# A graph-attention layer on one Trainium2 core: where the count and the report of failed rows stand, and the segment size for blocks 24 to 27

## The chip, the core and the metric

The kernel runs on one core of a Trainium2 chip. The metric is the device time of one launch in microseconds (us). Each kernel is run several times, and the median is used. One further execution is recorded by the hardware profiler. Times inside it are counted from the start of its span.

## The reference

There are 4096 nodes with 512 features. `adj` is a 4096 x 4096 matrix of f32; about one entry in 256 is not zero, and these are drawn between 0.05 and 1e9.

```python
ht = (h @ W).reshape(N, 4, 512).transpose(1, 0, 2)          # 4 heads
src = einsum('hnd,hd->hn', ht, a[:, :512, 0])
dst = einsum('hnd,hd->hn', ht, a[:, 512:, 0])
e = leaky_relu(src[:, :, None] + dst[:, None, :], 0.01) + adj[None]
h_prime = einsum('hij,hjd->hid', softmax(e, axis=-1), ht).mean(axis=0)
out = layernorm(x + h_prime)                                # over the 512 features
```

The entries of adj are added to the scores before the softmax. Where the largest entry of a row leads the second by more than the scores can make up, the softmax of that row is 1 at one column and 0 elsewhere, for all heads. The row of `h_prime` is then the row of x at that column times the mean of the four heads' W.

## The kernel before, in words

The kernel has two parts. `leading_rows` takes every row as one with such a lead, computes the output from that, and tests on the way whether the lead is large enough. `general` computes the whole attention for blocks of rows in which the test failed. A flag decides whether it is entered: `any_bad` is read by every engine at line 64, after `leading_rows`. In the profiled execution the flag is 0 and `general` does not run.

The rows are worked on in 32 blocks of 128. Row p * 32 + nb of the matrix lies in partition p of block nb. The order of the work is written out by hand: each engine executes its own instructions in the order of the source. A loop over t = 0 to 31 has a pipeline of these steps for each block:

- **Load.** SP loads the block's 128 x 4096 entries of adj (2 MB) up to five rounds ahead into one of six buffers. Blocks 28 to 30 come in two pieces and block 31 in four.
- **Segment maxima** (line 182, DVE). Each row is cut into segments of e columns, and the maximum of each segment is taken. For blocks 0 to 17 e is 16 (256 segments), for blocks 18 to 27 it is 32 (128 segments), for 28 to 31 it is 64 (64 segments).
- **Find the segment** (lines 189 and 191, DVE). MAX8 takes the eight largest segment maxima, and FIND_INDEX8 finds where they are. POOL makes a row number of it (198) and fetches that segment of adj anew from DRAM with an indirect DMA (202), into a tile named `lead`. The pool of such tiles has 8 buffers for e = 16, 8 for e = 32 and `LAST` for e = 64.
- **Find the column**, two rounds later (219 and 225, DVE). MAX8 of the fetched segment gives the second largest value inside it, and FIND_INDEX8 finds the maximum's column. For blocks 24 to 31 the MAX8 is left until after the loop. POOL adds the column up (227) and gathers the rows of x at these columns (213) into the tile y.
- **Turn and multiply**, three rounds later. PE transposes y in four pieces (240), ACT copies the result out of PSUM as yt (242), and PE multiplies it by the mean W in four steps of 128 (255). An f32 product is two passes in the profile. For blocks below 24 the block's own x is added by a product with the identity (248).
- **Layer norm and store.** ACT takes the sums for blocks 0 to 26 (277, 279), POOL makes the factor (282 to 284), ACT applies it (288). For blocks 27 to 31 DVE takes the statistics with BN_STATS (308, 312), ACT the square root (314), DVE the reciprocal (317), and DVE or ACT normalises (324, 288, 337). Blocks 24 to 27 are put by in a buffer of adj (268), and their x is added later (272).

After the loop stands the tail, a list of calls. Block 30's column (`find_column(NB - 2)`) waits for its fetched segment. Block 31's column is searched in the whole row (line 233, 4096 values). Its segment is fetched as well, but for the test alone. `test` (405 to 408) compares the lead of every row of all 32 blocks with a bound, and needs the segment of block 31. `count` (412) adds up over the partitions by a small product on PE, into a PSUM tile px. `report` is three small DVE instructions (416, 418, 419) that turn px into `n_bad` and `any_bad`. Block 31's products are made in two halves of 256 columns (297), and each half's statistics are taken as soon as it is there (331). The last store is that of block 31.

The part of the tail that the change touches reads in source order (before):

```python
    test()
    turn(NB - 2)
    ...
    products(NB - 3, KB - 1, KB)
    pg = count()
    products(NB - 2, 0, KB - 1)
    report(pg)
    moments(NB - 3)
    ...
    turn(NB - 1)
    products(NB - 2, KB - 1, KB)
```

Of the kernel before, what the change touches and what calls it, by code (L numbers as in the profile page):

```python
# [23 lines left out]
E_EARLY = 16  # L24
E_LAST = 64
EARLY = 18
LAST = 4


@with_exitstack  # L30
def gat_resnorm_kernel(
# [28 lines left out]
    any_bad = keep.tile([1, 1], I32, name="any_bad")  # L60

    leading_rows(tc, x, adj, W, a, out, ident, n_bad, any_bad)

    flag = nc.values_load(any_bad[0:1, 0:1], min_val=0, max_val=N)
# [5 lines left out]
def leading_rows(ctx, tc, x, adj, W, a, out, ident, n_bad, any_bad):  # L70
# [21 lines left out]
    lead_pool = ctx.enter_context(tc.tile_pool(name="lead_pool", bufs=1))  # L92
    LEADS = (8, 8, LAST)
    small = ctx.enter_context(tc.tile_pool(name="small", bufs=5))
# [3 lines left out]
    adj_rows = adj.rearrange("(p nb) m -> nb p m", nb=NB)  # L98
    spans = ((E_EARLY, 0, EARLY), (E, EARLY, NB - LAST), (E_LAST, NB - LAST, NB))
    adj_segs = {e: adj.rearrange("n (s e) -> (n s) e", e=e) for e, _, _ in spans}  # L100
# [135 lines left out]
    def turn(ib):  # L236
        y = y_t.pop(ib)
        tp = psum.tile([P, KB, P], F32, name="tp", bufs=2)
        for kb in range(KB):
            nc.tensor.transpose(tp[:, kb, :], y[:, ds(kb, P, KB)], ident)  # L240
        yt = yt_of[ib] = rows.tile([P, KB, P], F32, name="yt")
        nc.scalar.copy(yt, tp)  # L242
# [7 lines left out]
    def products(ib, lo=0, hi=KB):  # L250
        start = ib not in o_ps
        if start:
            o_ps[ib] = psum.tile([P, D], F32, name="o")
        for kb in range(lo, hi):
            nc.tensor.matmul(  # L255
                o_ps[ib], yt_of[ib][:, kb, :], w_sum[:, kb, :],
                start=(start and kb == 0), stop=(kb == KB - 1),
            )
# [11 lines left out]
    def add_x(engine, ib):  # L270
        o = o_ps[ib] = o_ps["by"][:, ib - BEHIND, :]
        engine.tensor_add(o, o, hold[:, ib, :])
# [13 lines left out]
    def finish(ib):  # L286
        i = slice(ib, ib + 1)
        nc.scalar.activation(hold[:, ib, :], o_ps.pop(ib), AF.Identity, bias=nm[:, i], scale=sd[:, i])  # L288
# [15 lines left out]
    def moments(ib):  # L304

        if ib < NB - 1:
            st = small.tile([P, nc.vector.BN_STATS_DIM], F32, name="st", bufs=2)
            nc.vector.bn_stats(st, o_ps[ib])
        else:
            st = halves_st  # L310
        mv = mean_var[ib] = small.tile([P, nc.vector.BN_AGGR_DIM], F32, name="mv", bufs=3)
        nc.vector.bn_aggr(mv, st)
        r = rt[ib] = sd[:, ib : ib + 1]
        nc.scalar.activation(r, mv[:, 1:2], AF.Sqrt, bias=eps)

    def factor(ib, shift=False):
        nc.vector.reciprocal(rt[ib], rt[ib])
        if shift:
            nc.vector.scalar_tensor_tensor(
                nm[:, ib : ib + 1], mean_var[ib][:, 0:1], -1.0, rt[ib], op0=OP.mult, op1=OP.mult  # L320
            )

    def normalise(ib, o, columns=slice(0, D)):
        nc.vector.tensor_scalar(
            hold[:, ib, columns], o, mean_var[ib][:, 0:1], rt[ib], op0=OP.subtract, op1=OP.mult
        )
# [3 lines left out]
    def stats_of_half(ib, k):  # L330
        nc.vector.bn_stats(halves_st[:, k, :], o_ps[ib][k])
# [78 lines left out]
    def count():  # L410
        pg = psum.tile([1, NB], F32, name="px", bufs=1)
        nc.tensor.matmul(pg, ones[:, 0:1], gap, start=True, stop=True)
        return pg

    def report(pg):
        nc.vector.tensor_scalar(n_bad, pg, -1.0, float(P), op0=OP.mult, op1=OP.add)
        total = once.tile([1, 1], F32, name="total")
        nc.vector.tensor_reduce(total, pg, axis=AX.X, op=OP.add)
        nc.vector.tensor_scalar(any_bad, total, -1.0, float(N), op0=OP.mult, op1=OP.add)
# [90 lines left out]
    stats(BEHIND + 2)  # L510
    rstd(slice(BEHIND, BEHIND + 3))
    products(NB - 3, KB - 1, KB)
    pg = count()
    products(NB - 2, 0, KB - 1)
    report(pg)
    moments(NB - 3)
    factor(NB - 3)
    normalise(NB - 3, o_ps.pop(NB - 3))
    turn(NB - 1)
    products(NB - 2, KB - 1, KB)  # L520
    add_x(nc.vector, LATE - 1)
    finish(BEHIND)
    finish(BEHIND + 1)
# [9 lines left out]
    stats_of_half(NB - 1, 0)  # L533
    factor(NB - 2)
    normalise(NB - 2, o_ps.pop(NB - 2))
    stats_of_half(NB - 1, 1)
    moments(NB - 1)
    factor(NB - 1, shift=True)
# [180 lines left out]
```

## Time and profile before

| | |
|---|---|
| median of 3 runs | 235.98 us (235.09 to 237.04) |
| the profiled execution | 235.12 us, span 233.6 us |
| PE busy | 165.8 us, 71% of the span |
| DVE busy | 199.2 us, 85% |
| ACT busy | 114.5 us, 49% |
| POOL busy | 102.0 us, 44% |
| DMA | 97.09 MB, mean 416 GB/s |
| mean granted PE clock | 0.965 of full speed |

The profiled execution took 1.5 us more than its span. A share of busy time is an average over the whole span. What holds the end is read from the chain of waits and the timelines of its last stage. In the rows, "out<-in" names what an instruction writes and reads, "x" counts instructions, and the part in brackets is the idle time of the engine before the instruction, with what ended it. PEld is PE's weight load, which runs beside the products. The ends of products are modelled, so they overlap a little; starts are the safer times.

### The profile page before, as it was taken

How to read it: one execution, taken by the hardware profiler on the slowest of the kernel's cores; microseconds unless marked ns; L12 is line 12 of the kernel's file. 1: busy time of each engine (PE TensorE's matmuls, PEld its weight loads, DVE VectorE, ACT ScalarE, POOL GpSimd, SP SyncE). 2: the span in 40 equal slices, each digit the busy share in tenths (PEclk: the TensorE clock that was granted, in tenths of full speed). 3: DMA queues.
4: the chain of work that ended last, by engine and by line, in shares of the span. 5: the costliest groups of instructions: out<-in, count | busy, mean ns of one | idle time of the engine just before them, and what ended most of it. 6: DMA issues, size and time to landing. Idle time of an engine off the chain costs nothing.

```text
span 233.6 us, 2053 instructions
## 1 busy us (share of the span) xinstructions
PE 165.8 (71%) x457; PEld 76.5 (33%) x457; DVE 199.2 (85%) x312; ACT 114.5 (49%) x284; POOL 102.0 (44%) x215
## 2 busy tenths in 40 slices
PE   0000001999978299979769689969999968999890
PEld 0000001344433244434325244324444433444360
DVE  0599999699919999999789995999999999979782
ACT  2012331055756159667547364643855644188661
POOL 2030334416424464646443552646464555457400
PEclk9999999999999679999999979988999999999997
DMA  6999999999999999999999999999999999999995
GB/s 242 434 429 428 432 408 422 435 435 420 434 422 435 419 436 422 430 422 436 426 428 431 426 428 422 425 432 426 423 436 417 425 427 424 412 423 424 422 387 219
DMA packets 11967, 97.09 MB, mean 416 GB/s; under 512 B 1960, under 2 KB 2408, under 8 KB 5936
## 3 DMA queue, kind: packets, MB, share of 16 engines
q1 hardware_dynamic: 8352, 88.08, 89.0%
q0 software_dynamic: 3584, 8.84, 9.6%
q8 instruction: 4, 0.07, 0.1%
q14 instruction: 11, 0.09, 0.1%
q10 hardware_dynamic: 16, 0.02, 0.0%
HBM read 88.54 MB, written 8.39 MB: 415 GB/s over the span
## 4 chain that ended last, share of the span: by engine, by line
POOL 34%; issue 34%; DMA 16%; DVE 9%; PE 3%; POOLq 1%; ACT 0%; SPq 0%; DVEq 0%
DMA adj_t<-in_adj_dram 11%; POOL lead L202 11%; POOL y L213 11%; DVE seg L182 6%; DMA lead<-in_adj_dram,row 5%; POOL sd L283 4%; POOL row L198 2%; POOL start L209 2%; POOL col L227 2%; PE o L255 2%; PE o L297 2%; POOL sd L282 1%; DVE col L233 1%; POOL nm L284 1%; DVE at L191 1%
## 5 line engine op out<-in xcount | busy, mean ns | idle before, releaser
L182 DVE TENSOR_REDUCE seg<-adj_t 128x128 f32<-128x2048 f32 (+3 forms) x66 | 145.4, 2207 | 21.8 <-DMA adj_t<-in_adj_dram 21.7
L255 PE MATMUL o<-w_sum,yt 128*128 128x512 f32 x248 | 118.9, 622 | 0.7 <-ACT yt L242 0.7
L255 PEld LDWEIGHTS o<-w_sum,yt 128*128 128x128 f32 x248 | 46.5, 199 | 64.6 <-issue 46.3
L240 PE MATMUL tp<-ident,y 128*128 128x128 f32 x128 | 23.1, 306 | 58.1 <-DMA y<-in_x_dram,col 57.7
L242 ACT COPY yt<-tp 128x512 f32<-128x512 f32 x32 | 18.8, 586 | 83.0 <-PE tp L240 83.0
L240 PEld LDWEIGHTS tp<-ident,y 128*128 128x128 f32 x128 | 19.1, 209 | 77.6 <-issue 75.9
L202 POOL DMA_INDIRECT lead<-in_adj_dram,row x32 | 32.7, 1022 | 15.0 <-POOL row L198 15.0
L213 POOL DMA_INDIRECT y<-in_x_dram,col x32 | 30.8, 961 | 16.9 <-POOL col L227 15.8
L248 PE MATMUL o<-hold,ident 128*128 128x512 f32 x52 | 29.4, 653 | 1.3 <-DMA hold<-in_x_dram 1.3
L198 POOL TENSOR_TENSOR row<-at,first 128x1 uint32<-128x1 uint32 x32 | 6.7, 209 | 44.7 <-DVE at L191 44.7
L227 POOL TENSOR_TENSOR col<-start,within 128x1 uint32<-128x1 uint32 x31 | 5.8, 188 | 33.5 <-DVE within L225 33.5
L262 ACT ACTIVATE sq<-hold 128x512 f32<-128x512 f32 x32 | 19.8, 619 | 0.0
L288 ACT ACTIVATE hold<-o,nm,sd 128x512 f32<-128x512 f32 x24 | 17.3, 771 | 1.2 <-POOL nm L284 1.2
L279 ACT ACTIVATE sq<-o,nm 128x512 f32<-128x512 f32 x24 | 16.5, 688 | 0.8
L277 ACT ACTIVATE sq<-o 128x512 f32<-128x512 f32 x24 | 14.4, 602 | 0.0
L347 ACT ACTIVATE w_sum<-w_sum 128x512 f32<-128x512 f32 x4 | 2.5, 629 | 20.8 <-DVE w_sum L346 20.8
L189 DVE MAX8 top<-seg 128x8 f32<-128x256 f32 (+2 forms) x32 | 11.6, 361 | 1.1
L191 DVE FIND_INDEX8 at<-top,seg 128x8 uint32<-128x256 f32 (+2 forms) x32 | 11.3, 352 | 0.0
L283 POOL TENSOR_TENSOR sd<-sd,power 128x2 f32<-128x2 f32 (+1 forms) x13 | 9.6, 735 | 1.1
L355 ACT ACTIVATE sq<-hold 128x512 f32<-128x512 f32 x16 | 9.9, 619 | 0.0
L248 PEld LDWEIGHTS o<-hold,ident 128*128 128x128 f32 x52 | 8.9, 211 | 3.0 <-DMA hold<-in_x_dram 2.5
L209 POOL TENSOR_TENSOR start<-at,width 128x1 uint32<-128x1 uint32 x31 | 6.6, 213 | 0.8
(84 smaller groups left out, 98.7 us busy)
## 6 DMA issues: line engine op xcount, KB each, us to landing
adj_t<-in_adj_dram SPq DMA_DIRECT2D x28, 2048.0 KB, 30.8
adj_t<-in_adj_dram SPq DMA_DIRECT2D x6, 1024.0 KB, 28.0
out_dram<-hold SPq DMA_DIRECT2D x6, 1024.0 KB, 17.3
hold<-in_L_gnn_W_dram SPq DMA_DIRECT2D x2, 2048.0 KB, 13.3
hold<-in_x_dram SPq DMA_DIRECT2D x2, 2048.0 KB, 37.7
hold<-in_x_dram SPq DMA_DIRECT2D x3, 1024.0 KB
adj_t<-in_adj_dram SPq DMA_DIRECT2D x4, 512.0 KB, 19.5
out_dram<-hold SPq DMA_DIRECT2D x3, 512.0 KB
```

Of the source, the lines that this page charges most:

```text
L182: nc.vector.tensor_reduce(seg_of[ib][:, ts(k, N // e // n)], adj_t[ib][:, ts(k, N // n)].rearrange("p (s e) -> p s e", e=e), axis=AX.X, op ...
L202: nc.gpsimd.indirect_dma_start(out=lead, out_offset=None, in_=adj_segs[e], in_offset=bass.IndirectOffsetOnAxis(ap=row[:, :1], axis=0),)
L213: nc.gpsimd.indirect_dma_start(out=y, out_offset=None, in_=x, in_offset=bass.IndirectOffsetOnAxis(ap=col[:, :1], axis=0),)
L240: nc.tensor.transpose(tp[:, kb, :], y[:, ds(kb, P, KB)], ident)
L242: nc.scalar.copy(yt, tp)
L248: nc.tensor.matmul(o_ps[ib], ident, hold[:, ib, :], start=start, stop=False)
L255: nc.tensor.matmul(o_ps[ib], yt_of[ib][:, kb, :], w_sum[:, kb, :], start=(start and kb == 0), stop=(kb == KB - 1),)
L262: nc.scalar.activation(sq, hold[:, ib, :], AF.Square, accum_out=xx[:, ib : ib + 1])
L277: nc.scalar.activation(sq, o, AF.Identity, scale=-1.0 / D, accum_out=nm[:, i])
L279: nc.scalar.activation(sq, o, AF.Square, bias=nm[:, i], accum_out=sd[:, i])
L283: nc.gpsimd.tensor_tensor(sd[:, i], sd[:, i], power[:, : i.stop - i.start], op=OP.pow)
L288: nc.scalar.activation(hold[:, ib, :], o_ps.pop(ib), AF.Identity, bias=nm[:, i], scale=sd[:, i])
```

## The change

Three edits. `count()` moves on PE from behind block 29's last product to behind block 30's last product. `report(pg)` moves on DVE from ahead of block 29's statistics to behind block 30's normalisation, just ahead of the statistics of block 31's second half. `LAST` becomes 8, so that blocks 24 to 27 are searched in 64 segments of 64 columns, fetch segments of 64 columns, and the pool of such tiles has 8 buffers.

```diff
-LAST = 4
+LAST = 8
...
     products(NB - 3, KB - 1, KB)
-    pg = count()
     products(NB - 2, 0, KB - 1)
-    report(pg)
     moments(NB - 3)
     factor(NB - 3)
     normalise(NB - 3, o_ps.pop(NB - 3))
     turn(NB - 1)
     products(NB - 2, KB - 1, KB)
+    pg = count()
     add_x(nc.vector, LATE - 1)
...
     stats_of_half(NB - 1, 0)
     factor(NB - 2)
     normalise(NB - 2, o_ps.pop(NB - 2))
+    report(pg)
     stats_of_half(NB - 1, 1)
     moments(NB - 1)
```

ACT and SP keep their instructions in their order. On DVE and PE no instruction is added or taken away; in blocks 24 to 27 the tiles of the search change their sizes.

## The prediction

> **What bounds the kernel now.** I read the page first (engines, slices, DMA), then the chain that ended last over its last 57 us, then the timelines of PE, ACT and DVE in the last 20 us, the search's rows kept apart by shape, the gathers' landing times, and the busy time by stage.
>
> The stages say that the stream of transfers is the limit until about 225 us, and that something else sets the last 8 us (columns: stretch, length, busy us of PE, PEld, DVE, ACT, POOL, clock, DMA share, GB/s):
>
> ```profile
> 195.00:205.00 10.00, 9.05 (x26) 3.68 (x24) 9.43 (x18) 2.71 (x5) 4.71 (x9) 1.00 1.01 417
> ...
> 220.00:225.00 5.00, 4.89 (x17) 2.39 (x16) 4.04 (x11) 2.40 (x7) 1.27 (x3) 1.00 1.01 420
> 225.00:230.00 5.00, 3.12 (x15) 2.41 (x13) 3.88 (x13) 3.25 (x8) 0.00 (x0) 1.00 0.86 346
> 230.00:233.60 3.60, 0.00 (x0) 0.00 (x0) 0.01 (x1) 0.15 (x1) 0.00 (x0) 0.64 0.35 134
> ```
>
> The chain of waits, in order of time (start, us, what), names what that is:
>
> ```profile
> 204.11 5.79 DMA lead<-in_adj_dram,row
> ...
> 210.25 2.36 DVE col L233 x2
> 212.61 6.04 DMA lead<-in_adj_dram,row
> 218.68 0.24 DVE inner L219
> ...
> 219.90 0.22 PE px L412 x2
> 220.12 2.77 PE o L255 x6
> 222.89 0.11 issue
> 223.00 0.72 PE tp L240 x4
> 223.72 0.86 PE o L255 x2
> 224.58 3.55 PE o L297 x16
> ```
>
> Read forward: the gather of block 31's segment ends at 218.65, the test of the leads follows, PE counts (L412), and only then come block 30's products, block 31's transposes (L240) and its products in halves (L297). So the chain does pass through the count. But the small piece "222.89 0.11 issue" is where a second chain may end at the same moment, and the chain shows only one. The transposes at 223.00 read the gathered rows y of block 31. The answer for the tile y between 214 and 224 us has one gather, and how long it took:
>
> ```profile
> L213 POOL DMA_INDIRECT y<-in_x_dram,col x1: 958/958/958, 215.5 to 215.5; - x1
> DMA to landing us min/median/max: 7.4/7.4/7.4
> ```
>
> The timelines give the rest (start, us, engine, line, what; in brackets the idle time before and what ended it):
>
> ```profile
> 215.51 0.96 POOL L213 DMA_INDIRECT y<-in_x_dram,col  x1 [0.64 <-PE o L255]
> 218.09 0.72 PE L240 MATMUL tp<-ident,y 128*128 128x128 f32 x4 [0.52 <-DMA y<-in_x_dram,col]
> 218.64 1.02 PE L255 MATMUL o<-w_sum,yt 128*128 128x512 f32 x2
> 219.90 0.22 PE L412 MATMUL px<-gap,ones 128*1 128x32 f32 x2 [0.23 <-DVE gap L408]
> 223.56 1.02 PE L255 MATMUL o<-w_sum,yt 128*128 128x512 f32 x2
> 223.76 0.59 ACT L242 COPY yt<-tp 128x512 f32<-128x512 f32 x1 [2.00 <-PE tp L240]
> 227.07 0.55 DVE L324 TENSOR_SCALAR hold<-hold,mv,sd 128x512 f32<-128x512 f32 x1
> 228.16 0.43 DVE L331 BATCH_NORM_STATS2 halves_st<-o 128x6 f32<-128x256 f32 x1 [0.54 <-PE o L297]
> ```
>
> Block 31's rows land at 215.51 + 7.4 = 222.91. Block 30's gather left at 211.16 and took 6.8 us (same view, 210 to 213 us), so its rows landed at 217.96 and PE turned them at 218.09, 0.13 later, with PE idle. Block 31's turn at 223.00 is 0.09 after its landing. It starts as soon as its rows are there: **two chains end together at 223.00**, one through the count, one through the rows of block 31. Shortening one of them alone moves nothing.
>
> For the third edit, the search's rows by shape, and the place where DVE last waited for adj on the way to block 30:
>
> ```profile
> L189 DVE MAX8 top<-seg 128x8 f32<-128x128 f32 x10 | 3.0, 295 | 0.3
> L189 DVE MAX8 top<-seg 128x8 f32<-128x64 f32 x4 | 0.9, 228 | 0.1
> 182.27 2.29 DVE L182 TENSOR_REDUCE seg<-adj_t 128x64 f32<-128x2048 f32 x1 [0.29 <-DMA adj_t<-in_adj_dram]
> ```
>
> **What the Trainium skill says.** "Perfetto Trace Analysis", Roofline: one core alone is held by its 16 DMA engines, about 435 GB/s. The stages agree: 417 to 430 GB/s at a share of 1.00 to 1.01 wherever the stream is full. The same page, Sequencer Loop: an engine's instructions go into its queue in order, and each waits there for its semaphores. The trace agrees: the count waits for L408, and the products behind it, whose input L242 was done at 218.84 + 0.59 = 219.43, start at 220.05. "DMA: Bandwidth & Descriptors", Why small descriptors are slow: a piece costs its bytes over 32 in cycles plus 3. A lead of 128 B is then 7 cycles and one of 256 B is 11. No view prices one piece; the leads of 256 B issued at 204.1 and 212.6 landed in 5.8 and 6.0 us, beside a median of 6.2 over all 32 leads, so the larger piece isn't seen.
>
> **The change part by part.**
>
> *Count behind block 30's last product.* On PE, block 29's last product starts at 218.64; such a product holds PE 0.86 us (223.56 to 224.42, where L297 starts), so PE is free at 219.50. It now sits until 219.90 for the test and counts until 220.05. After the change the three products of block 30 start at 219.50 (their copy is done at 219.43). They gain 0.55 us, and PE is free for block 31's turn at 222.89 - 0.55 = 222.34 instead of 222.89. Its rows are still there only at 222.91, so the turn stays at 223.00: **gain 0**, and PE idles there instead. From below: if the rows came before 222.3, the gain would be the 0.55.
>
> The count itself now stands between block 30's last product and L297. In before, L297 starts at 224.42, and both its inputs end there: PE is free at 224.42, and the copy L242 ends at 224.35, after which PE starts 0.07 later, as it did after block 29's copy (213.67 + 0.59, start at 214.33). So there is no idle time to hide the count in. Its cost start to start is 219.90 to 220.05 = 0.15. Bounds: "TensorE: Matmul & The Clock Gate", Wait — 56ns, not 53.3ns?, gives about 25 ns as the least from one small matmul to the next, which for the two passes shown (x2) is an estimate of 0.05; above, the row's whole 0.22. I take **+0.15**, since the weights of L297 have to be loaded behind the count's as they were in before.
>
> *Report ahead of block 31's second half.* Three DVE instructions (L416, L418, L419) leave 220.16 to 220.54, together with the 0.31 us that L416 waited for the count. Block 29's statistics start up to 0.6 earlier; what is late next is the addition for block 30, which waits for its last product at 224.62, as before. Blocks 28 and 29 are stored earlier than 222.83, into a stream that is full until 225. In the new place they take 0.38 start to start, between the end of L324 at 227.62 and L331 at 228.16, where DVE now idles 0.54 us; with the count's 0.15 the idle time becomes 0.69. **Cost 0**, 0.3 us to spare. Without that cover it is +0.38, since L331, the square root, the last normalisation and the last store (issued at 230.18, landed 2.4 later) are all behind it. Every engine reads the flag after its own last work; SP, the last, after 230.5, so a flag at 228.0 instead of 220.6 holds up none that ends the kernel.
>
> *Blocks 24 to 27 in 64 segments.* From MAX8's start to the next block's reduction is 0.68 us with 128 values (186.94 to 187.62) and 0.55 with 64 (197.47 to 198.02): 4 x 0.13 = 0.53 less on DVE. The search inside the segment grows from 0.17 (189.80 to 189.97) to 0.20 (200.20 to 200.40), in rounds 26 to 29: +0.03 each. But DVE waits 0.29 at 182.27 for block 27's adj, and that time is the stream's. What is saved in rounds 24 to 26 becomes a longer wait there. Behind it remain -0.13 (round 27) and +0.09 (rounds 27 to 29): -0.04. That does lie on the second chain, because block 30's lead (204.11 + 5.8) ends a DVE wait at 210.00, ahead of the index search whose result is block 31's gather. Against it: 128 rows x 128 B more in each of four gathers are 65.5 KB, 0.15 us at 427 GB/s, half of it ahead of block 27's adj: up to +0.08. I take **0**. Bounds: -0.35 (DVE's wait at 210.00 was 0.34; beyond it block 31's own adj decides), +0.15. The four MAX8 of the later leads (L219) grow by 0.03 each, 0.13 in all, ahead of the 0.24 us that the last one waits for its gather: hidden.
>
> *Sum.* 0 + 0.15 + 0 + 0 = +0.15 us. The profiled execution took 235.12 (span 233.6 and 1.5 outside it), so 235.27. The median of the three runs, 235.98, lies 0.86 above that execution; the same step on it gives **236.1**.
>
> **The rivals.**
>
> *The rows of block 31 come early (faster).* The three gathers of x before it took 6.3, 6.9 and 6.8 us to land; 7.4 is the longest of the four. With 6.8 the rows land at 222.31, only the count's chain was the bound, and the change gives -0.55 + 0.15 = -0.4: 235.6. For it: the spread of landings, and that the chain runs through L412. Against: the execution at hand.
>
> *The search's savings reach the end too (faster).* If DVE does not wait for block 27's adj in a usual execution, the saved 0.53 - 0.12 shortens the way to block 30's lead by up to 0.35: -0.4 - 0.35 = -0.75, 235.2. For it: that wait is only 0.29. Against: transfers are at their ceiling in every stage, and DVE waits again at 207.76 (0.47) for the last piece of adj.
>
> *The report stands in the way (slower).* DVE becomes last in the tail: L416 to L419 run just ahead of L331. It decides as soon as block 30's normalisation ends later than 227.9 (0.3 us later than now), or the count is read later than that. Then up to 0.38 comes on top of 0.15, with 0.07 more for a count at its dearest: +0.6, 236.6. For it: DVE is busy 3.88 of the 5 us from 225 on. Against: the 0.54 us of idle time in just that place.
>
> **How the numbers follow.** Forecast 0.55, early rows 0.24, search too 0.08, report 0.13. All cases lie between 235.2 and 236.6. With the unknown costs at both ends and the scatter of the runs (235.09 to 237.04 around 235.98) 8 in 10 is 234.9 to 236.9. About 1% is what a measurement of this kernel can tell from no change; that is 2.4 us, and no case reaches it. I leave 0.04 on either side for what the views don't show, such as a lower granted clock in the last products (16 passes, 3.7 us).
>
> **What would show it.** Right: the count's idle time is gone from PE, block 30's first product starts near 219.5, and the turn L240 of block 31 now shows a wait of about 0.5 us for y; L412 lies right ahead of L297; DVE's idle time ahead of L331 is mostly filled by L416 to L419; DVE waits longer for adj in round 27. Wrong: the turn of block 31 starts earlier after its gather's issue without waiting for y, L331 starts at once behind L419, or DVE runs through rounds 24 to 30 with no wait for adj.

## The result, and the profile after

The changed kernel takes 239.5 us (239.11 to 240.13 in 6 runs) against 235.53 us (235.01 to 237.38 in 6 runs) for the kernel before: a ratio of 1.0155 with an interval of 1.0111 to 1.0199. The forecast was 236.1, so the change is slower by 4.0 us where +0.15 was expected. The profiled execution took 239.51 us with a span of 237.9 (before: 235.12 and 233.6).

The busy time by stage of the kernel after (columns as in the prediction) shows at once where the time is not:

```profile
220.00:225.00 5.00, 4.34 (x15) 1.92 (x14) 3.47 (x8) 2.31 (x7) 1.63 (x3) 1.00 1.01 420
225.00:230.00 5.00, 3.43 (x16) 2.67 (x15) 3.91 (x16) 2.98 (x8) 0.00 (x0) 1.00 0.86 350
230.00:233.60 3.60, 0.00 (x0) 0.00 (x0) 0.32 (x1) 0.46 (x1) 0.00 (x0) 0.59 0.38 138
233.60:237.90 4.30, 0.00 (x0) 0.00 (x0) 0.00 (x0) 0.00 (x0) 0.00 (x0) 0.50 0.00 0
```

Up to 233.6 the stages look like those of before. Then come 4.30 us in which no engine computes and nothing is transferred. Most of the loss stands behind the landing of the last store. The timeline of PE after reads, from the start of block 30's turn:

```profile
218.15 0.72 PE L240 MATMUL tp<-ident,y 128*128 128x128 f32 x4 [0.54 <-DMA y<-in_x_dram,col]
218.71 3.68 PE L255 MATMUL o<-w_sum,yt 128*128 128x512 f32 x8
223.05 0.72 PE L240 MATMUL tp<-ident,y 128*128 128x128 f32 x4 [0.66 <-DMA y<-in_x_dram,col]
223.61 1.02 PE L255 MATMUL o<-w_sum,yt 128*128 128x512 f32 x2
224.56 0.22 PE L412 MATMUL px<-gap,ones 128*1 128x32 f32 x2
224.71 3.72 PE L297 MATMUL o<-w_sum,yt 128*128 128x256 f32 x16
```

Block 30's products now follow block 29's last one in one row of eight passes. Block 31's turn starts at 223.05, as before, and now shows a wait of 0.66 us for y. The count lies right ahead of L297, and L297 starts 0.29 later than before (224.42). DVE around the report, in its timeline after:

```profile
227.27 0.55 DVE L324 TENSOR_SCALAR hold<-hold,mv,sd 128x512 f32<-128x512 f32 x1
227.73 0.17 DVE L416 TENSOR_SCALAR n_bad<-px 1x32 int32<-1x32 f32 x1
227.83 0.17 DVE L418 TENSOR_REDUCE total<-px 1x1 f32<-1x32 f32 x1
228.04 0.14 DVE L419 TENSOR_SCALAR any_bad<-total 1x1 int32<-1x1 f32 x1
228.47 0.43 DVE L331 BATCH_NORM_STATS2 halves_st<-o 128x6 f32<-128x256 f32 x1 [0.29 <-PE o L297]
```

In before, the last of the three and POOL's last work are these rows:

```profile
220.47 0.14 DVE L419 TENSOR_SCALAR any_bad<-total 1x1 int32<-1x1 f32 x1
...
222.23 0.19 POOL L284 TENSOR_TENSOR nm<-nm,sd 128x3 f32<-128x3 f32 x1
```

So the flag is done at 228.18 instead of 220.61. The report fits ahead of L331 with 0.29 us to spare. The last store is issued at 230.49, against 230.18 before. So the computation is 0.3 us later, and the rest of the 4 us is elsewhere.

It is found among the instructions that the page does not count as busy. The view of single lines shows them: engine (a "q" marks its sequencer), operation, count, ns least/median/most, and the first and last start in us. For L64 (every engine reads the flag), L65 (the branch over `general`) and L714 (the closing of the kernel), here of **before**:

```profile
L64 POOLq TENSOR_LOAD <-any_bad x1: 521/521/521, 222.2 to 222.2; - x1
...
L65 POOLq INC_SWDGE_SEM  x1: 1476/1476/1476, 223.7 to 223.7; - x1
...
L714 POOLq DRAIN  x3: 40/103/5306, 225.2 to 233.3; - x3
...
L714 SPq DRAIN  x3: 7/7/7, 232.7 to 233.0; - x3
```

and of **after**:

```profile
L64 POOLq TENSOR_LOAD <-any_bad x1: 1013/1013/1013, 228.2 to 228.2; - x1
...
L65 POOLq INC_SWDGE_SEM  x1: 1476/1476/1476, 230.2 to 230.2; - x1
...
L714 POOLq DRAIN  x3: 40/103/5306, 231.7 to 237.6; - x3
...
L714 SPq DRAIN  x3: 7/7/7, 233.6 to 237.3; - x3
```

POOL has a closing of its own behind the read of the flag: the branch, some semaphore waits, an INC_SWDGE_SEM of 1.48 us, and a DRAIN of 5.31 us (the first of its three, which starts at 225.2 and at 231.7). From the end of the flag's read to the end of that DRAIN it is 7.81 us in both kernels: 222.71 to 230.52 before, 229.23 to 237.04 after. In after, SP's wait at the end is over at 237.2, right behind that DRAIN. Before, SP, whose last store had to land, was the last at 232.77 (the end of its second DRAIN), and POOL had 2.25 us of slack. After, SP is there at 233.71 and waits for POOL until 237.04. POOL's closing moved by 6.52; 6.52 less the 2.25 of slack is 4.27, and the span grew by 4.3.

SP too is there 0.94 us later than before: 0.31 is the later issue of the last store, and 0.64 its landing, which took 3.08 us instead of 2.44. POOL's closing covers this, but without it these 0.9 us would have stayed.

The waits of SP's queue show the place, but with a wrong name (us in total, times, longest); before, then after:

```profile
SPq L714 <- PEq L714: 0.7, 2, 0.5
```

```profile
SPq L714 <- PEq L714: 4.1, 2, 3.5
```

PE's own closing had started at 230.1 in after, with DRAINs of 8 ns. A wait for several semaphores is put down to one of them; the 5.31 us row shows which it was. The chain that ended last does not help here: in after its last piece is ACT's normalisation (L337) at 229.90, 8 us ahead of the end, because it follows instructions that compute.

### The profile page after: what moved, and what is told of

Read it like the earlier page. It is cut to its first block, busy times and chain, and to the rows that moved or that the text cites. A ratio compares the mean times of both kernels' runs of the same rounds, so it can differ in the third digit from the quotient of the medians.

```text
span 237.9 us, 2054 instructions
## 1 busy us (share of the span) xinstructions
PE 164.1 (69%) x457; PEld 75.7 (32%) x457; DVE 198.9 (84%) x312; ACT 114.3 (48%) x284; POOL 102.7 (43%) x215
## 4 chain that ended last, share of the span: by engine, by line
POOL 34%; issue 33%; DMA 17%; DVE 9%; PE 2%; POOLq 1%; ACT 0%; SPq 0%; DVEq 0%
DMA adj_t<-in_adj_dram 11%; POOL lead L202 11%; POOL y L213 11%; DVE seg L182 6%; POOL sd L283 4%; DMA y<-in_x_dram,col 3%; DMA lead<-in_adj_dram,row 2%; POOL row L198 2%; POOL start L209 2%; POOL col L227 2%; PE o L297 2%; DVE col L233 1%; POOL sd L282 1%; POOL nm L284 1%; DVE at L191 1%
## 5 line engine op out<-in xcount | busy, mean ns | idle before, releaser
L255 PE MATMUL o<-w_sum,yt 128*128 128x512 f32 x248 | 116.5, 612 | 0.7 <-ACT yt L242 0.7
L255 PEld LDWEIGHTS o<-w_sum,yt 128*128 128x128 f32 x248 | 45.8, 196 | 63.9 <-issue 44.9
```

The source lines that it names most:

```text
L255: nc.tensor.matmul(o_ps[ib], yt_of[ib][:, kb, :], w_sum[:, kb, :], start=(start and kb == 0), stop=(kb == KB - 1),)
```

## The experiments

Two theories stood after the first comparison. **A, POOL's closing:** the flag's lateness acts only through POOL, whose closing of 7.8 us starts when it reads the flag. **B, the late count and report:** they cost the computation itself, or a late flag holds up every engine. A third was open beside them: **C, the segment size** of blocks 24 to 27. The table is from the traces (us from the start of each span; "flag read" is the end of POOL's read; "SP there" is SP's first DRAIN of the closing). The sections below give the runs.

| kernel | flag read by POOL | POOL's long DRAIN | SP there | span | ratio to before |
|---|---|---|---|---|---|
| before | 222.71 | 225.21 to 230.52 | 232.7 | 233.6 | |
| e7 | 223.58 | 226.09 to 231.39 | 232.7 | 233.6 | 1.001 [0.9991, 1.0028] |
| e3 | 226.30 | 228.79 to 234.10 | 233.8 | 234.9 | 1.0052 [1.0036, 1.0069] |
| e2 | 228.90 | 231.39 to 236.69 | 233.5 | 237.5 | 1.017 [1.0153, 1.0187] |
| after | 229.23 | 231.73 to 237.04 | 233.6 | 237.9 | 1.0155 [1.0111, 1.0199] |
| e4b | 231.53 | 234.03 to 239.34 | 234.7 | 240.2 | 1.0234 [1.0164, 1.0305] |

### e1 and e2: the change in two parts

e1 is before with the segment size alone, e2 is before with the two moves alone.

```diff
-LAST = 4
+LAST = 8
```

> The segment size alone (LAST = 8), with the count and the report where they were before. Theory (POOL's close): POOL reads the flag any_bad late, and only then starts its own end of about 7.8 us; the segment size has no part in it, so the time stays within 0.3 us of before. Rival (larger segments): if the 256 B gathers cost the 4 us, this kernel is about 4 us slower than before.

> The two moves alone, LAST = 4. Theory (POOL's close): the whole loss is here, about +4 us against before, and POOL is again the engine that comes last, some 3.5 us behind the last store. Rival (larger segments): no change. Rival (the tail's products and statistics are late): +0.3 us, since the last store is issued only 0.3 later.

e1 took 235.3 us, a ratio of 1.0008 [0.9993, 1.0023]; e2 took 239.05, 1.017 [1.0153, 1.0187]. The whole loss is in the moves, and theory C falls. In e2 the last store is issued at 230.17, as early as in before, and the span is 3.9 longer all the same.

### e3: the report a few instructions sooner

The count stays where the change puts it. The report goes up past block 30's statistics.

```diff
     o_ps[NB - 2] = hold[:, NB - 2, :]
+    report(pg)
     moments(NB - 2)
...
     normalise(NB - 2, o_ps.pop(NB - 2))
-    report(pg)
```

> The changed kernel with the count where it is, and the report right behind block 30's addition on DVE instead of behind its normalisation: the flag is ready at about 225.8 instead of 228.2. Theory (POOL's close): the end follows the flag one for one, so about 2.3 us come back and the kernel is about 1.6 to 2 us slower than before. Rival (the flag is read behind PE's or DVE's late work, wherever it stands): about +4 us as in the changed kernel.

It took 236.36 us, 1.0052 [1.0036, 1.0069]. The flag is done at 225.76 instead of 228.18, 2.4 us sooner, and the span is 234.9 instead of 237.9. The rows of e3:

```profile
L714 POOLq DRAIN  x3: 44/103/5306, 228.8 to 234.6; - x3
...
L714 SPq DRAIN  x3: 7/7/7, 233.8 to 234.4; - x3
```

POOL's read of the flag ended 2.93 us sooner than in after (226.30 against 229.23; the read itself took 0.51 instead of 1.01), its DRAIN 2.94 sooner, and the span is 2.95 shorter. So the end follows POOL's read, and more came back than the 2.3 that was expected. POOL's DRAIN ends at 234.10 and SP is there at 233.83: the two are nearly level, and most of the 1.2 us that remain are SP's own lateness.

### e7: the report inside the slack

Before, with the report moved down past block 29's normalisation only, which makes the flag 2.4 us later than in before (223.04).

```diff
     products(NB - 2, 0, KB - 1)
-    report(pg)
     moments(NB - 3)
     factor(NB - 3)
     normalise(NB - 3, o_ps.pop(NB - 3))
+    report(pg)
```

> The kernel before with the report alone moved on DVE, to behind block 29's normalisation: the flag is ready at about 222.5 instead of 220.6. Theory (POOL's close): POOL itself is busy until 222.4 and its close ends 2.2 us ahead of SP, so a flag up to about 224.4 costs nothing: within 0.3 us of before. Rival (the end follows the flag from the start, one for one): +1.9 us.

It took 235.43 us, 1.001 [0.9991, 1.0028]. POOL had only just done its own last work, so it read the flag 0.87 us later than in before, and its DRAIN ended at 231.39, still ahead of SP at 232.7. A later flag is free as long as POOL's closing is not last.

### e4 and e4b: POOL late, the flag early

To part "POOL reads late" from "the flag is late", POOL gets one small instruction that waits for block 31's second half, and the count and the report stay as in before. First with a tile of its own:

```diff
     stats_of_half(NB - 1, 1)
+    late = once.tile([P, 1], F32, name="late")
+    nc.gpsimd.tensor_scalar(late, halves_st[:, 1, 0:1], 1.0, 0.0, op0=OP.mult, op1=OP.add)
```

> The kernel before, with its flag as early as before (220.6), and one small POOL instruction more that waits for the statistics of block 31's second half (about 228.6); its result is used by nothing. Theory (POOL's close): POOL reads the early flag only after that instruction, at about 228.9, and its end of 7.8 us follows: about +4.5 us against before. Rival (a late flag holds up the branches or the instruction fetch of all engines): the flag is early here, so no change beyond 0.3 us.

It took 243.71 us, 1.0368 [1.0351, 1.0385]: 8.5 us more, where about half was expected. About half of it was lost before the tail. The last store is issued at 234.27, 4.1 later than in before, and the stages of e4 show a slower stream:

```profile
60.00:90.00 30.00, 22.31 (x57) 10.06 (x56) 23.54 (x37) 15.36 (x41) 12.86 (x28) 0.89 1.01 419
```

Before moves 428 GB/s there. The new tile takes 4 bytes in each partition. The source up to this stage is the same, so presumably it is the place of the buffers behind the tile that differs; that was not shown. So e4's time says nothing clean on the two theories. Its trace does show the flag done at 224.79, and yet POOL's long DRAIN ending at 241.35, with SP there at 237.08. The instruction was made to write into an existing tile:

```diff
     stats_of_half(NB - 1, 1)
+    nc.gpsimd.tensor_scalar(power[:, 0:1], halves_st[:, 1, 0:1], 1.0, 0.0, op0=OP.mult, op1=OP.add)
```

> The same question as in the kernel with one late POOL instruction, now without a new tile: the instruction writes a column of POOL's own table power, which nothing reads any more, so that no buffer changes its place. The flag stays early (220.6); POOL's last instruction waits for the statistics of block 31's second half (about 228.6). Theory (POOL's close): POOL reads the flag at about 228.9, its close of 7.8 us follows, about +4.3 us against before, with the last store issued at the same time as before (230.2). Rival (a late flag holds up all engines): no change beyond 0.3 us.

It took 241.81 us (239.52 to 242.2), 1.0234 [1.0164, 1.0305]. The same stage is back at its rate:

```profile
60.00:90.00 30.00, 23.54 (x62) 10.54 (x62) 24.52 (x37) 17.54 (x46) 13.78 (x30) 0.94 1.01 428
...
200.00:205.00 5.00, 5.00 (x11) 2.24 (x10) 4.86 (x9) 1.17 (x2) 2.26 (x6) 0.66 1.02 415
```

But this execution's tail came 2 us later than before's: the last store is issued at 232.25, where 230.2 was expected. The delay comes in at block 26. Its turn waited longer for y, whose gather took 8.0 us to land where before's took 6.6. PE's rows, before and then e4b:

```profile
197.63 0.72 PE L240 MATMUL tp<-ident,y 128*128 128x128 f32 x4 [0.95 <-DMA y<-in_x_dram,col]
```

```profile
199.57 0.82 PE L240 MATMUL tp<-ident,y 128*128 128x128 f32 x4 [2.41 <-DMA y<-in_x_dram,col]
```

Behind that wait PE was granted half its clock, from 200.0 to 203.4 us (mean 0.66 in the stage; before has 1.00 there). How much of the 2 us each of the two costs isn't separated. The other three runs left no trace, so why they took 239.52 to 242.2 stays open; the one at 239.52 is 4.3 above before's median of that series, 235.24, which is the price that was expected. The closing in the profiled execution does not depend on it:

```profile
L65 POOLq INC_SWDGE_SEM  x1: 1476/1476/1476, 232.5 to 232.5; - x1
...
L715 POOLq DRAIN  x3: 40/103/5306, 234.0 to 239.9; - x3
...
L715 SPq DRAIN  x3: 7/7/7, 234.7 to 239.6; - x3
```

Again 7.81 us from the flag's read (231.53) to the DRAIN's end (239.34), while SP was there at 234.70, 4.6 us sooner (in after, 3.4 sooner). Here the flag was done at 223.04. So a late POOL at an early flag is enough to make the end wait for it, by about as much as in after. Theory B does not explain that.

### e5 and e6: what the closing makes up for

`general`, which does not run, issues its DMAs on POOL, and the INC_SWDGE_SEM with the waits beside it stands at the line of the branch that skips it. In e5 (after) and e6 (before) these DMAs are issued on SP instead, at six places like this one:

```diff
-        nc.gpsimd.dma_start(adj_t, adj[ds(ib, P, NB), :])
+        nc.sync.dma_start(adj_t, adj[ds(ib, P, NB), :])
```

> The changed kernel, with the DMAs of the part that is not run here (general) issued by SP instead of POOL; the instructions of the part that runs are the same. Theory (POOL's close): POOL's 7.8 us are the price of making up, on the path past general, for the counts of the POOL-issued DMAs that general would have made; without such DMAs the close is short and the kernel ends with SP's last store: about +0.3 us against before. Rival (the close is what any POOL queue costs at the end): POOL still takes 7.8 us from the flag, and the kernel stays at about +4.

> The kernel before, with general's DMAs issued by SP instead of POOL. Theory (POOL's close): in before the close ends about 2.2 us ahead of SP, so taking it away gains nothing: within 0.3 us of before. Rival (the close also burdens the last store or the final barrier): faster by 0.5 us or more.

e5 took 237.56 us, 1.0085 [1.0057, 1.0113]; e6 took 235.94, 1.0026 [1.0005, 1.0047]. In e5 the INC_SWDGE_SEM and four waits beside it are gone, but the DRAIN is not:

```profile
L714 POOLq DRAIN  x3: 40/103/5306, 229.5 to 235.3; - x3
...
L714 SPq DRAIN  x3: 7/7/7, 234.2 to 235.0; - x3
```

The expectation that nearly everything comes back fell. From the end of the flag's read to the end of the DRAIN it is now 5.97 us instead of 7.81, so what stood at the branch for these DMAs is about 1.8 us; the DRAIN of 5.3 is not made by `general`'s DMAs. In e6 POOL is done at 227.84, far ahead of SP, and nothing is won: the closing is only paid for when it is last. e6 is even 0.7 us slower than before, more than the 0.3 allowed for. The edit is not free for SP, which now has nine semaphore waits at the branch instead of one and is at its closing 0.82 us behind the last landing instead of 0.09. The same holds for e5.

### e8: the DRAIN taken early

After, with one instruction more on POOL, right behind its last piece of work in the tail:

```diff
     rstd(slice(BEHIND, BEHIND + 3))
+    nc.gpsimd.drain()
     products(NB - 3, KB - 1, KB)
```

> The changed kernel with one DRAIN more on POOL, right behind POOL's last work at about 222.5 and so ahead of its reading of the flag at 228.2. Open is what the 5.3 us of POOL's last DRAIN are. Theory A (it is work left over from the kernel, done once): the early DRAIN takes the 5.3 us beside the tail, the last one is short, and POOL ends at about 231.7, ahead of SP: about +0.3 us against before. Theory B (every such DRAIN at that place costs 5.3 us, whatever came before): the last DRAIN stays at 5.3 us and the kernel at about +4.

It took 236.25 us, 1.004 [1.0024, 1.0057]. In this expectation A and B are two readings of the DRAIN. The rows of e8 show the first, that the long DRAIN is there once and is not a price of ending:

```profile
L512 POOLq DRAIN  x1: 6088/6088/6088, 223.6 to 223.6; - x1
...
L65 POOLq INC_SWDGE_SEM  x1: 185/185/185, 231.5 to 231.5; - x1
...
L715 POOLq DRAIN  x3: 34/50/103, 231.8 to 234.7; - x3
```

The early DRAIN takes 6.09 us beside the tail. Its row starts while POOL's last work (L284) still runs, and it ends 5.32 us behind the end of that work (229.70 and 224.38), so it is as long as the one at the end of before. Then INC_SWDGE_SEM takes 0.19 instead of 1.48, and the closing DRAIN 0.05 instead of 5.31. POOL is done at 231.82, and SP, at 234.1, ends the kernel again. Of the 4.0 us, about 3 come back, where all but 0.3 was expected. So the strict form of this part's theory of POOL's closing, that the late flag acts through nothing else, is not shown: about 1 us remains with POOL out of the way, as in e3. In the trace it lies with SP: the last store was issued 0.75 later than in before and took 3.1 us to land instead of 2.4. After (3.1) and e5 (3.3) show such landings too, but so does e1 (2.9), whose flag is early and which is not slower. What makes them isn't settled.

### e9 and e10: both kernels without the flag

Both leave out the same part: the reading of the flag, the branch and the recomputation of failed rows. The hint that announces the branch goes with it. The count and the report still run, early in e10 and late in e9.

```diff
-    flag = nc.values_load(any_bad[0:1, 0:1], min_val=0, max_val=N)
-    with tc.If(flag > 0, preferred_fallthrough_block=True, label="general"):
-        general(tc, x, adj, W, a, out, ident, n_bad)
...
-        if t == NB // 2:
-            tc.mark_branch_hint_location("general", engines=HINTED)
```

> The changed kernel without general and without the branch and the reading of the flag (the recomputation of failed rows is left out). The count and the report still run at their late places. Theory (POOL's end waits for the flag): POOL's last DRAIN now starts at 222.5 and ends at about 227.8, SP ends the kernel, and against its partner without the moves it is +0.3 us. Rival (the late count and report themselves hold up PE, DVE or the last store): still +4 us against its partner.

> The partner: the kernel before without general, the branch and the reading of the flag (the recomputation of failed rows is left out). Theory (POOL's end has 2.2 us to spare in before): within 0.5 us of before. Rival (the branch is a cost of its own in before): faster by 1 us or more.

e9 (after) took 235.04 us, 0.9989 [0.9974, 1.0005]; e10 (before) took 235.02, 1.0001 [0.9986, 1.0017]. POOL's DRAIN in e9 and then in e10, where nothing waits for a flag:

```profile
L709 POOLq DRAIN  x3: 45/102/5903, 222.6 to 232.9; - x3
```

```profile
L709 POOLq DRAIN  x3: 45/102/5547, 223.2 to 233.5; - x3
```

In e9 it starts at 222.59 and is over at 228.49. With the flag gone, the changed order costs nothing that can be measured. This is the cleanest cut between the theories: the late count and report cost nothing measurable on PE and DVE, and the loss exists only where the flag is read.

### e11: the count where PE does not wait

PE waited 0.23 us for the test ahead of the count in before. Here one product of block 30 is put ahead of the count, so that the wait is filled, and the flag stays early.

```diff
-    pg = count()
-    products(NB - 2, 0, KB - 1)
+    products(NB - 2, 0, 1)
+    pg = count()
+    products(NB - 2, 1, KB - 1)
     report(pg)
```

> The kernel before with the count moved on PE behind the first of block 30's products, and the report where it is on DVE. PE no longer waits for the test, and the flag is ready at about 221, inside POOL's slack. Theory (two chains end together at block 31's turn): PE is free earlier but waits for block 31's rows, no change beyond 0.2 us. Rival (the chain through the count alone sets the end, as the chain view shows it): 0.4 us faster.

It took 235.24 us, 0.9991 [0.9974, 1.0008]. PE's timeline in e11:

```profile
221.48 0.22 PE L412 MATMUL px<-gap,ones 128*1 128x32 f32 x2
221.62 1.98 PE L255 MATMUL o<-w_sum,yt 128*128 128x512 f32 x4
224.14 0.72 PE L240 MATMUL tp<-ident,y 128*128 128x128 f32 x4 [0.53 <-DMA y<-in_x_dram,col]
```

The count's wait is gone, and what is late next is block 31's gather: the turn waits 0.53 us for y (landed at 224.00; this whole execution ran about 1 us later). The interval reaches down to 0.6 us faster, so the time alone does not exclude the rival's 0.4; the wait for y in the timeline speaks against it, in one execution. e9 against e10 says the same of the whole move without the harm: there is nothing to gain that can be measured. None of these kernels is measurably faster than the kernel before.

## Why the prediction was wrong, point by point

- **The step that failed** stands at the end of the part on the report: "Every engine reads the flag after its own last work; SP, the last, after 230.5, so a flag at 228.0 instead of 220.6 holds up none that ends the kernel." The times in it are right (228.18; SP reads at 230.9). But it asked who *reads* last, and not what each engine still has to do *behind* the read. In before, POOL's last row of work started at 222.23; its read of the flag ended at 222.71, and it had 7.81 us of closing left, none of which counts as busy. The term was put at 0. The closing moved by 6.52, had 2.25 of slack, and so moved the end by 4.27. Had POOL not been last, SP alone would still have been 0.94 later, where the forecast had 0.15. e3 and e7 show the size with a flag that is late by other amounts, e4b without a late flag, e9 and e10 with none.
- **No rival had it.** The slower one put DVE into the way of L331 with at most +0.6. The report fits there with 0.29 us to spare, near the forecast of 0.3. The signs named for being right nearly all came: the wait for y, the count right ahead of L297, the report in DVE's idle time. They watched the computation, and the loss was behind it.
- **Two chains at 223.00** held. The turn started at 223.05 with a wait of 0.66 for y, whose gather took 7.5 us in after. e11 shows the same with the count elsewhere.
- **The count, +0.15,** was right in kind and somewhat small. Start to start it is 0.15 again (224.56 to 224.71), but L297 is 0.29 later: 0.05 is the turn, and 0.09 lies between block 30's last product and the count, so in this place it cost 0.24, a little over the upper bound of 0.22. The last store is 0.31 later. In e9 against e10 it isn't measurable.
- **The segment size, 0,** held: 1.0008 in e1. What DVE saves does become a wait for adj, but one round sooner than told. In after it waits 0.32 us at 176.62, where before shows no such wait, and 0.25 at 182.21, where before has 0.29. The 7 and 11 cycles a piece in the prediction are an estimate; no run prices a piece.
- **The Trainium skill.** The rule that the prediction took from "Perfetto Trace Analysis", Sequencer Loop, was not applied where it counted: POOL's closing is queued behind its read of the flag. The same page, Sequencer-only Instruction (DRAIN, etc), says that the profile's duration of a DRAIN is its execution, without the semaphore wait ahead of it. The runs agree: the 5.31 us row isn't a wait for another engine, since it is just as long at 225.2 as at 234.0, and 0.05 after an early drain. It can hold the end of the engine's own work: the longer rows of e8, e9 and e10 end 5.32 us behind POOL's last work.

## What to carry to other kernels

When a value that every engine reads at the end is moved, write down for each engine what is queued behind the read, down to the last DRAIN, and compare those ends with the last store's landing; rows that aren't "busy" count. An engine that is done early may hold the longest closing, and its slack (here 2.25 us) is the budget for the move. If a late flag can't be avoided, an early drain on POOL put that closing beside other work here and gave back about 3 of the 4 us (e8).

## What the runs showed of the hardware

- POOL's first closing DRAIN took 5.31 us in every kernel that read the flag and had not drained before. The rows of 6.09 (e8, the early one), 5.90 (e9) and 5.55 us (e10) start while POOL's last work runs, and end 5.32 behind it. After the early drain the closing one took 0.05. These kernels issue 64 gathers on POOL; that the DRAIN belongs to them was not tried, and what is done in it stays open.
- In e4, where a tile of 4 bytes per partition is allocated in the pool `once`, the stream moved 419 GB/s from 60 to 90 us, against 428 in before and in e4b, and the last store came 4.1 us later than in before. What in the tile does that was not looked into.
- The traces show stretches of 3.4 or 6.8 us in which PE is granted half its clock. The three that begin near 200 us follow a long wait of PE for y: 2.41 us in e4b (stretch at 200.0), 2.01 in e8 (198.8) and 2.60 in e10 (199.3). Before waited 0.95 there and has none. e7 also waited 2.0 us there, and has none either, so such a wait did not always bring one.
